# Finishing batches inside the attention loops, a last projection in three parts, and a first chunk in two loads: two cross-attention layers on one core

## The chip, the core and the metric

The kernel runs on one core of a Trainium2 chip. The core has five engines that run side by side, each through its own queue in order: TensorE (matrix products and transposes, PE in the profile, with its weight loads shown apart as PEld), VectorE (DVE), ScalarE (ACT), GpSimd (POOL) and SyncE (SP, which here only issues DMAs). The metric is the device time of one execution in microseconds; smaller is better.

## What is computed

Eight batches of 100 queries with 1024 features pass through two cross-attention layers against the same 1444 context rows of 512 features. All of it is fp32.

```python
def _L0_xattn_ref(query, key, Wq, bq, Wk, bk, Wv, bv, Wo, bo):
    Q = query @ Wq + bq; K = key @ Wk + bk; V = key @ Wv + bv
    weights = softmax(Q @ K.T * scale, axis=-1)
    return query + (weights @ V) @ Wo + bo

def _L1_xattn_ref(emb, latent, Wq, bq, Wk, bk, Wv, bv, gamma, beta):
    q = emb @ Wq + bq; k = latent @ Wk + bk; v = latent @ Wv + bv
    w = softmax(q @ k.T * scale, axis=1)          # over the 100 queries
    x = w @ v + emb
    return (x - mean(x)) * rsqrt(var(x) + 1e-6) * gamma + beta
```

## The kernel before

The program multiplies weights first (Wq with Wk, Wv with Wo), so that keys and values are never formed: scores are a product with the raw context, and the weighted rows of the raw context are projected afterwards. Large products are made from seven half-size products of sums (`half_product`, line 116, is called by all of them).

The stages in order of time: products of weights (`weight_products` for "qk0", "vo0", "qk1"); queries of layer 0; a loop over the eight batches for layer 0, in which scores of batch b + 2 and weighted rows of batch b alternate on TensorE; the projection of layer 0; queries of layer 1; the same kind of loop for layer 1 (lines 780 to 818); and the end of the last batch.

TensorE's instructions run in the order in which the program writes them. The other engines' instructions are put in order by a scheduler, which takes the earliest written of those that are ready by its own estimate; that order is then fixed. Semaphores hold an instruction until its inputs are there and its output buffer is free.

*First chunk.* `weight_products` (lines 179 to 287) works on eight chunks, `units[0]` to `units[7]`, of 128 rows: 1024 columns of the left factor (WqT) and 512 of the right one (WkT). For "qk0" the first half of the left columns and all right columns of each chunk are loaded in turn (lines 191 to 194), chunk 0's left half through ACT's queue and all else through SP's; the left factor's second halves follow (lines 195 to 197). The first product X (line 257) takes the first half of the left columns (four blocks of 128) and the first half of the right ones (256) of chunks 0 to 3, the second, Z, those left columns of chunks 4 to 7, and the third, Y, sums that VectorE makes of second halves (lines 259 and 260). On its queue VectorE also has sums of right chunks scaled by a bias (line 254, `accumulate`). Eight matrix products of ones warm the array up (line 87).

*Layer 1's end.* The loop over b runs 48 steps; for b = 6 and b = 7 a step is one product of the weighted rows (line 446). ScalarE then copies these rows from PSUM (line 457), and `weight_totals` (line 617) transposes a row of totals. Batches 0 to 4 are projected together after b = 4's rows are there, at the end of the loop of b = 5 (`project1_halves`, G1 = 5); batches 5 and 6 together by `project1` at the end of b = 6; batch 7 by `project_last`. A projected batch is ended by `finish`: TensorE transposes eight blocks of it into two banks of PSUM, VectorE adds the value bias from there (line 689) and takes statistics (lines 694 and 699), GpSimd takes the power -0.5 (line 702), VectorE scales and shifts (lines 703 and 707), and GpSimd issues the output (line 708). Batches 0 and 1 are finished at the end of b = 5, batches 2, 3 and 4 at the end of b = 6 ahead of `project1`, and 5 and 6 behind it.

`bank` hands out six banks of PSUM in turn to transposes, totals and projections; a bank can be written again when its reader, mostly VectorE, is done. Rows `z` have three buffers.

Of the kernel before, what the change touches and what calls it, by code (L numbers as in the profile page):

```python
# [24 lines left out]
F32 = mybir.dt.float32  # L25
AF = mybir.ActivationFunctionType
ALU = mybir.AluOpType
# [23 lines left out]
def two_layer_cross_attention(ctx: ExitStack, tc: tile.TileContext, a: dict, out: bass.AP):  # L51
# [127 lines left out]
    def weight_products(name, left, right, l_width, r_width, scaled):  # L179

        H, lh, rh = EC // 2, l_width // 2, r_width // 2
        nb, per = lh // P, 512 // rh
        lsrc = a[left].rearrange("(p c) n -> p c n", c=EC)
        rsrc = a[right].rearrange("(p c) n -> p c n", c=EC)
        units = [unit(f"{name}_{h}") for h in range(EC)]
        if name == "qk0":  # L190
            for h in range(EC):
                first = h == 0
                (nc.scalar if first else nc.sync).dma_start(out=units[h][:, :lh], in_=lsrc[:, h, :lh])
                nc.sync.dma_start(out=units[h][:, l_width:], in_=rsrc[:, h, :])
            for i in range(H):
                for h in (i, H + i):
                    nc.sync.dma_start(out=units[h][:, lh:l_width], in_=lsrc[:, h, lh:])
        else:
            for h in range(EC):
                nc.sync.dma_start(out=units[h][:, :l_width], in_=lsrc[:, h, :])  # L200
                nc.sync.dma_start(out=units[h][:, l_width:], in_=rsrc[:, h, :])

        def lefts(k, j):
            return [units[k * H + i][:, j * lh : (j + 1) * lh] for i in range(H)]

        def rights(k, j):
            return [units[k * H + i][:, l_width + j * rh : l_width + (j + 1) * rh] for i in range(H)]

        A11, A12, A21, A22 = lefts(0, 0), lefts(1, 0), lefts(0, 1), lefts(1, 1)
        B11, B12, B21, B22 = rights(0, 0), rights(0, 1), rights(1, 0), rights(1, 1)  # L210
        extra = [work.tile([P, LC * G1 * T], F32, tag="AT", name=f"{name}_s{n}", bufs=2) for n in range(2)]
        S1 = [extra[i // 2][:, i % 2 * 768 : i % 2 * 768 + lh] for i in range(H)]
        T1 = [extra[i // 2][:, i % 2 * 768 + lh : (i % 2 + 1) * 768] for i in range(H)]

        dst = weights.tile([P, l_width // P, r_width], F32, tag="w", name=name)

        def pair(n):
            return [(bank2 if n == "w" else bank)(f"{name}_{n}{j}") for j in range(2)]

        def product(banks, lhs, rhs, fresh):  # L220
            half_product(banks, lhs, rhs, fresh, nb, rh)

        def block(r, c, j):

            n = r * nb + j * per
            return dst[:, n : n + per, c * rh : (c + 1) * rh]

        def put(r, c, banks):
            for j in range(2):
                nc.scalar.copy(block(r, c, j), banks[j].rearrange("p (n w) -> p n w", n=per))  # L230

        def add(r, c, banks):
            for j in range(2):
                to = block(r, c, j)
                nc.vector.tensor_tensor(to, to, banks[j].rearrange("p (n w) -> p n w", n=per), ALU.add)

        accs = {}

        def accumulate(side):
            for v, of in scaled:  # L240
                if of != side:
                    continue
                width = (l_width, r_width)[side]
                if width == E:
                    acc = row(f"{name}_{v}")
                else:
                    acc = work.tile([P, L], F32, tag="half", name=f"{name}_{v}", bufs=1)
                accs[v] = acc
                for h in range(EC):
                    src = units[h][:, :l_width] if side == 0 else units[h][:, l_width:]  # L250
                    if h == 0:
                        nc.vector.tensor_scalar(acc, src, cols[v][:, h : h + 1], None, ALU.mult)
                    else:
                        nc.vector.scalar_tensor_tensor(acc, src, cols[v][:, h : h + 1], acc, ALU.mult, ALU.add)  # L254

        X = pair("x")
        product(X, A11, B11, True)
        put(0, 0, X)
        combine(T1, B12, B11, ALU.subtract)
        combine(S1, A21, A22, ALU.add)  # L260
        Z = pair("z")
        product(Z, A12, B21, True)
        accumulate(1)
        add(0, 0, Z)
        Y = pair("y")
        product(Y, S1, T1, True)
        put(1, 1, Y)
        combine(B11, B22, T1, ALU.subtract)
        T2 = B11
        combine(B21, B21, T2, ALU.subtract)  # L270
        W = pair("w")
        product(W, A22, B21, True)
        put(1, 0, W)
        combine(S1, S1, A11, ALU.subtract)
        S2 = S1
        combine(B12, B22, B12, ALU.subtract)
        product(X, S2, T2, False)
        put(0, 1, X)
        accumulate(0)
        combine(A21, A11, A21, ALU.subtract)  # L280
        combine(A12, A12, S2, ALU.subtract)
        product(X, A21, B12, False)
        add(1, 0, X)
        add(1, 1, X)
        product(Y, A12, B22, False)
        add(0, 1, Y)
        return dst, [accs[v] for v, _ in scaled]
# [377 lines left out]

        seven_products("o1", A, Bs, S, T_, 4, n, add, add, right=lambda k: right_sums(Bs, T_, (k,)))

    def project1(b0, n, A):

        t0, t1 = b0 * T, (b0 + n) * T  # L670
        for e in range(EC):
            ps = bank(f"o1_{b0}_{e}")
            for k in range(LC):
                nc.tensor.matmul(
                    ps[:, : n * T], wv1[:, k, e * P : (e + 1) * P], A[:, k, : n * T], start=(k == 0), stop=(k == LC - 1)
                )
            to = xT[:, e, t0:t1]
            nc.vector.tensor_tensor(to, to, ps[:, : n * T], ALU.add)

    def untransposed(s):  # L680

# [6 lines left out]
            half = slice(j * 512, (j + 1) * 512)  # L688
            nc.vector.scalar_tensor_tensor(z[:, half], bv1[:T, half], s["r"], ps[:T, :], ALU.mult, ALU.add)

    def statistics(s, j):
        if j == 0:
            s["stats"] = small.tile([T, 2, 6], F32, tag="stats", name=f"stats_{s['b']}")
        nc.vector.bn_stats(s["stats"][:, j, :], s["z"][:, j * 512 : (j + 1) * 512])

    def normalise(s):
        b, z = s["b"], s["z"]
# [12 lines left out]
    def finish(s):  # L710
        untransposed(s)
        for j in range(2):
            statistics(s, j)
        normalise(s)

    def project_last(s, A):

        for j in range(2):
            ps = bank(f"ol_{j}")
            half = slice(j * 512, (j + 1) * 512)  # L720
            for k in range(LC):
                nc.tensor.matmul(ps[:T, :], A[:, k, :T], wv1[:, k, half], start=(k == 0), stop=(k == LC - 1))
            nc.vector.tensor_tensor(s["z"][:, half], s["z"][:, half], ps[:T, :], ALU.add)
            statistics(s, j)
        normalise(s)


# [49 lines left out]
    c1.append(key_bias1(1))  # L777
    weight_sums(batches[0])
    A1 = {}
    for b in range(B):  # L780
        nxt = b + 2 < B
        if b in (0, G1, B - 1):
            n = {0: G1, G1: 2, B - 1: 1}[b]
            t = work.tile([P, LC * G1 * T], F32, tag="AT", name=f"A1T_{b}", bufs=2)
            t = t[:, : LC * n * T].rearrange("p (c t) -> p c t", c=LC)
            for i in range(n):
                A1[b + i] = (t, t[:, :, i * T : (i + 1) * T])
        c, *cT = loaded(load_rows(b), *([load_columns(b + 2)] if nxt else []))
        if nxt:
            A = attend1(batches[b], c)  # L790
            s1 = scores1(batches[b + 2], *cT, c1[(b + 2) // G])
        else:
            A = weighted_rows(batches[b]["w"], c, A1[b][1], f"A1_{b}")
            s1 = iter(())
        for n in range(MC * LC):
            next(s1, None)
            next(A)
            if n == 10 and 1 <= b <= B - 2:
                attended(batches[b - 1], A1[b - 1][1])
        weight_totals(batches[b])  # L800
        if b == B - 1:
            untransposed(batches[b])
        if b + 1 < B:
            weight_sums(batches[b + 1])
        if b == 1:
            AS = project1_sums(wv1)
        if b == G1:
            project1_halves(*AS, A1[0][0])
            for d in range(2):
                finish(batches[d])  # L810
        if b == B - 2:
            for d in range(2, G1):
                finish(batches[d])
            project1(G1, 2, A1[G1][0])
            for d in range(G1, B - 1):
                finish(batches[d])
        if b == B - 1:
            project_last(batches[b], A1[b][0])

# [23 lines left out]
```

## Time and profile before

| | us |
|---|---|
| median of 3 runs (666.31 to 668.25) | 666.34 |
| the profiled execution | 666.33 |
| its span, first to last instruction | 664.4 |
| first matrix product starts | 5.22 |
| first `finish` starts on TensorE | 604.44 |
| loop of batch 6 on TensorE, its totals | 617.33 |
| loop of batch 7 on TensorE, its totals | 647.47 |
| last matrix product ends | 655.59 |

A line of the profile's timeline gives the start and the length in us, the engine, the line of the kernel, the operation, what it writes and reads, shapes, a count, and in brackets the idle time of the engine ahead of it and what ended it. A line of the waits gives who waited for whom, the sum in us, how often, and the longest. One matrix product of fp32 is two instructions in the trace; a transpose is one. POOL's spans are rough. The engines' busy shares are means over the whole span and hide what a stage is limited by.

### The profile page before, as it was taken

The page shows a single profiled execution, that of the slowest core. Times are in us where ns is not written, and L with a number is a line of the kernel's source. Part 1 is how long each engine was busy: PE and PEld are TensorE (multiplying, and loading weights), DVE is VectorE, ACT ScalarE, POOL GpSimd, SP SyncE. Part 2 cuts the span into 40 slices and gives each one's busy share as a digit, 9 for nine tenths or more (in the row PEclk, how much of TensorE's full clock was granted, in tenths as well). Part 3 has the DMA queues.
Part 4 walks back from the last instruction along what each step waited for, and adds up shares of the span by engine and source line. Part 5 has one row for each costly group of instructions (what it writes and reads, how often), then busy time and mean ns, then how long its engine had stood idle before and what let it go on. Part 6 is the DMA issues. An engine that isn't in the chain of part 4 may idle for free.

```text
span 664.4 us, 10317 instructions
## 1 busy us (share of the span) xinstructions
PE 651.4 (98%) x4352; PEld 551.6 (83%) x4352; DVE 359.2 (54%) x649; ACT 101.2 (15%) x295; POOL 22.8 (3%) x31
## 2 busy tenths in 40 slices
PE   9999999999999999999999999999999999999894
PEld 8885445568899999999998555589999999989891
DVE  5979638996055123321232874269344443468884
ACT  1110100331101111101120000213322323210000
POOL 2000000000000000000000000000000000001330
PEclk9999999999999999999999999999999999999998
DMA  9936046000199688888999003038899889900221
GB/s 298 373 117 265 0 135 239 1 0 1 48 340 316 247 291 291 299 288 304 326 331 325 2 0 127 1 111 260 289 312 308 290 292 315 316 15 12 64 75 49
DMA packets 59946, 127.51 MB, mean 192 GB/s; under 512 B 3896, under 2 KB 22328, under 8 KB 59900
## 3 DMA queue, kind: packets, MB, share of 16 engines
q1 hardware_dynamic: 57598, 119.82, 52.9%
q0 software_dynamic: 2048, 6.56, 3.0%
q8 instruction: 34, 0.56, 0.4%
q10 hardware_dynamic: 254, 0.47, 0.2%
q14 instruction: 12, 0.10, 0.0%
HBM read 123.56 MB, written 3.28 MB: 191 GB/s over the span
## 4 chain that ended last, share of the span: by engine, by line
PE 95%; DVE 2%; DMA 1%; issue 0%; POOLq 0%; POOL 0%; DVEq 0%
PE A L446 15%; PE s L476 12%; PE s L573 11%; PE A L629 10%; PE qk_x L116 6%; PE g_x L116 5%; PE qk_y L116 4%; PE o_x L116 4%; PE g_y L116 3%; PE vo_x L116 3%; PE o_y L116 3%; PE qk_w L116 2%; PE qk_z L116 2%; PE vo_y L116 2%; PE g_w L116 2%; PE g_z L116 2%
## 5 line engine op out<-in xcount | busy, mean ns | idle before, releaser
L446 PE MATMUL A<-w,c 120*128 120x100 f32 x960 | 145.4, 268 | 0.0
L446 PEld LDWEIGHTS A<-w,c 120*128 120x128 f32 x960 | 128.6, 191 | 0.1
L573 PE MATMUL s<-g1T,cT 128*120 128x100 f32 (+1 forms) x768 | 123.2, 261 | 0.0
L476 PE MATMUL s<-cT,g0T 128*100 128x131 f32 (+1 forms) x704 | 122.8, 275 | 0.0
L629 PE MATMUL A<-c,w 120*100 120x128 f32 (+1 forms) x576 | 110.7, 273 | 0.0
L573 PEld LDWEIGHTS s<-g1T,cT 128*120 128x120 f32 (+1 forms) x768 | 105.1, 185 | 0.6 <-issue 0.3
L476 PEld LDWEIGHTS s<-cT,g0T 128*100 128x100 f32 x704 | 87.7, 167 | 0.0
L629 PEld LDWEIGHTS A<-c,w 120*100 120x100 f32 (+1 forms) x576 | 74.0, 168 | 0.0
L488 DVE TENSOR_SCALAR p<-s,c 100x394 f32<-100x394 f32 (+2 forms) x32 | 18.8, 594 | 89.6 <-PE s L476 89.4
L593 ACT ACTIVATE w<-w,negmax 120x100 f32<-120x100 f32 (+1 forms) x96 | 35.1, 366 | 75.3 <-DVE negmax L591 75.3
L583 DVE SCALAR_TENSOR_TENSOR w<-s,c 120x400 f32<-120x400 f32 (+1 forms) x24 | 13.8, 573 | 41.6 <-PE s L573 41.6
L116 PE MATMUL qk_x<-qk 128*128 128x256 f32 x128 | 28.9, 384 | 0.4 <-DMA qk<-in_L_xattn_WkT 0.4
L116 PEld LDWEIGHTS qk_x<-qk 128*128 128x128 f32 x128 | 24.2, 192 | 4.7 <-DMA qk<-in_L_xattn_WqT 0.6
L508 ACT COPY w<-pT 120x400 f32<-120x400 f32 (+1 forms) x24 | 11.6, 493 | 100.0 <-PE pT L507 100.0
L702 POOL TENSOR_TENSOR rstd<-rstd,mhalf 100x1 f32<-100x1 f32 x8 | 11.8, 1478 | 233.7 <-DVE rstd L701 233.7
L596 DVE RECIPROCAL rtotal<-total 120x4 f32<-120x4 f32 (+1 forms) x24 | 4.2, 176 | 28.2 <-ACT w L593 28.2
L492 ACT ACTIVATE p<-p,negmax 100x1444 f32<-100x1444 f32 x8 | 12.0, 1499 | 47.2 <-DVE negmax L490 47.2
L515 DVE TENSOR_TENSOR xT<-xT,o_x 128x400 f32<-128x400 f32 (+1 forms) x24 | 13.7, 602 | 8.3 <-PE o_x L116 8.0
L254 DVE SCALAR_TENSOR_TENSOR qk_L_xattn_bk<-qk,L_xattn_bk,qk_L_xattn_bk 128x1024 f32<-128x1024 f32 x14 | 17.9, 1279 | 0.0
L593 ACT ACTIVATION_READ_ACCUMULATOR w<-w,negmax 120x1 f32 (+1 forms) x96 | 17.9, 186 | 0.0
L610 DVE TENSOR_REDUCE part<-w 120x100 f32<-120x1100 f32 x8 | 17.2, 2147 | 0.0
L319 DVE SCALAR_TENSOR_TENSOR kb<-xT,wqbk,kb 128x400 f32<-128x400 f32 x28 | 16.9, 628 | 0.2
(198 smaller groups left out, 861.3 us busy)
## 6 DMA issues: line engine op xcount, KB each, us to landing
c<-in_ctx SPq DMA_DIRECT2D x48, 768.0 KB, 7.8
cT<-in_ctxT SPq DMA_DIRECT2D x32, 728.0 KB, 7.0
cT<-in_ctxT SPq DMA_DIRECT2D x32, 722.0 KB, 6.5
c<-in_ctx SPq DMA_DIRECT2D x16, 512.0 KB, 8.2
qk<-in_L_xattn_WkT SPq DMA_DIRECT2D x16, 256.0 KB, 6.3
vo<-in_L_xattn_Wo SPq DMA_DIRECT2D x8, 512.0 KB, 7.2
qk<-in_L_xattn_WqT SPq DMA_DIRECT2D x8, 512.0 KB
qk<-in_L_xattn_WqT SPq DMA_DIRECT2D x15, 256.0 KB, 5.4
```

Source lines behind the costliest of these rows:

```text
L116: nc.tensor.matmul(banks[n // per][:, n % per * width : (n % per + 1) * width], lhs[i][:, n * P : (n + 1) * P], rhs[i], start=(fresh and i ...
L254: nc.vector.scalar_tensor_tensor(acc, src, cols[v][:, h : h + 1], acc, ALU.mult, ALU.add)
L319: nc.vector.scalar_tensor_tensor(acc, src, wqbk[:, k : k + 1], acc, ALU.mult, ALU.add)
L446: nc.tensor.matmul(ps[:, k * T : (k + 1) * T], c[m // CQ][:r, m % CQ, k * P : (k + 1) * P], w[:r, m, :], start=(m == 0 and k == 0), stop=( ...
L476: nc.tensor.matmul(banks[n // PM][:T, CUTS[n] - o : CUTS[n + 1] - o], q0[:, k, t0 : t0 + T], cT[k][:, CUTS[n] : CUTS[n + 1]], start=(k == ...
L488: nc.vector.tensor_scalar(p[:, o:e], ps[:T, : e - o], SCALE, c0[:, b : b + 1], ALU.mult, ALU.add)
L515: nc.vector.tensor_tensor(to, to, ps[:, : n * width].rearrange("p (n t) -> p n t", n=n), ALU.add)
L573: nc.tensor.matmul(ps[:r, (m - m0) * T : (m - m0 + 1) * T], cT[m // CQ][:, k, o : o + r], q1[:, k, t0 : t0 + T], start=(k == 0), stop=(k = ...
L583: nc.vector.scalar_tensor_tensor(w[:r, grp, :], ps[:r, :GT].rearrange("p (c t) -> p c t", t=T), SCALE, c1[:r, t0 : t0 + T].unsqueeze(1).to ...
L593: nc.scalar.activation(w[:r, m, :], w[:r, m, :], AF.Exp, bias=negmax[:r, m : m + 1], accum_out=total[:r, m : m + 1])
L610: nc.vector.tensor_reduce(part[:MR], w[:MR, :last, :].rearrange("p c t -> p t c"), AX.X, ALU.add)
L629: nc.tensor.matmul(ps[:T, part], w[:r, m, :], c[m // CQ][:r, m % CQ, part], start=(m == 0 and k == 0), stop=(m == MC - 1), skip_group_chec ...
```

## The change

Three edits are made.

1. `finished` names the steps at which batches are finished. In the loop of b = 6 batches 0, 1, 2 and 3 come behind steps 0, 12, 26 and 40; batch 4 comes in the middle of `project1`, behind its fourth block of columns; batches 5 and 6 come behind steps 0 and 16 of the loop of b = 7. The calls at the loops' ends go.
2. `project_last` makes columns 0 to 511, 512 to 895 and 896 to 1023 one after the other, each with its add and statistics, in place of two halves.
3. For "qk0" chunk 0's left half is loaded by two DMAs of 256 columns on ACT's queue; its right half by two DMAs of 256 columns on SP's, the second of which comes behind chunk 1's loads.

```diff
         if name == "qk0":
-            for h in range(EC):
-                first = h == 0
-                (nc.scalar if first else nc.sync).dma_start(out=units[h][:, :lh], in_=lsrc[:, h, :lh])
+            for part in (slice(0, lh // 2), slice(lh // 2, lh)):
+                nc.scalar.dma_start(out=units[0][:, part], in_=lsrc[:, 0, part])
+            nc.sync.dma_start(out=units[0][:, l_width : l_width + rh], in_=rsrc[:, 0, :rh])
+            for h in range(1, EC):
+                nc.sync.dma_start(out=units[h][:, :lh], in_=lsrc[:, h, :lh])
                 nc.sync.dma_start(out=units[h][:, l_width:], in_=rsrc[:, h, :])
+                if h == 1:
+                    nc.sync.dma_start(out=units[0][:, l_width + rh :], in_=rsrc[:, 0, rh:])
...
-    def project1(b0, n, A):
+    def project1(b0, n, A, between):
...
             nc.vector.tensor_tensor(to, to, ps[:, : n * T], ALU.add)
+            if e == EC // 2 - 1:
+                between()
...
-    def statistics(s, j):
+    def statistics(s, j, part, parts):
         if j == 0:
-            s["stats"] = small.tile([T, 2, 6], F32, tag="stats", name=f"stats_{s['b']}")
-        nc.vector.bn_stats(s["stats"][:, j, :], s["z"][:, j * 512 : (j + 1) * 512])
+            s["stats"] = small.tile([T, parts, 6], F32, tag=f"stats{parts}", name=f"stats_{s['b']}")
+        nc.vector.bn_stats(s["stats"][:, j, :], s["z"][:, part])
...
-        for j in range(2):
+        parts = (slice(0, 512), slice(512, 896), slice(896, E))
+        for j, part in enumerate(parts):
+            n = part.stop - part.start
             ps = bank(f"ol_{j}")
-            half = slice(j * 512, (j + 1) * 512)
             for k in range(LC):
-                nc.tensor.matmul(ps[:T, :], A[:, k, :T], wv1[:, k, half], start=(k == 0), stop=(k == LC - 1))
-            nc.vector.tensor_tensor(s["z"][:, half], s["z"][:, half], ps[:T, :], ALU.add)
-            statistics(s, j)
+                nc.tensor.matmul(ps[:T, :n], A[:, k, :T], wv1[:, k, part], start=(k == 0), stop=(k == LC - 1))
+            nc.vector.tensor_tensor(s["z"][:, part], s["z"][:, part], ps[:T, :n], ALU.add)
+            statistics(s, j, part, len(parts))
...
+    finished = {(B - 2, n): (d,) for d, n in enumerate((0, 12, 26, 40))}
+    finished.update({(B - 1, 0): (G1,), (B - 1, 16): (G1 + 1,)})
...
                 attended(batches[b - 1], A1[b - 1][1])
+            for d in finished.get((b, n), ()):
+                finish(batches[d])
...
             project1_halves(*AS, A1[0][0])
-            for d in range(2):
-                finish(batches[d])
         if b == B - 2:
-            for d in range(2, G1):
-                finish(batches[d])
-            project1(G1, 2, A1[G1][0])
-            for d in range(G1, B - 1):
-                finish(batches[d])
+            project1(G1, 2, A1[G1][0], lambda: finish(batches[G1 - 1]))
```

More of the change, by code (lines that the diff above doesn't have):

```diff
@@ L712, in finish @@
         for j in range(2):
-            statistics(s, j)
+            statistics(s, j, slice(j * 512, (j + 1) * 512), 2)
         normalise(s)
     def project_last(s, A):
-        for j in range(2):
+        parts = (slice(0, 512), slice(512, 896), slice(896, E))
+        for j, part in enumerate(parts):
+            n = part.stop - part.start
             ps = bank(f"ol_{j}")
-            half = slice(j * 512, (j + 1) * 512)
             for k in range(LC):
-                nc.tensor.matmul(ps[:T, :], A[:, k, :T], wv1[:, k, half], start=(k == 0), stop=(k == LC - 1))
-            nc.vector.tensor_tensor(s["z"][:, half], s["z"][:, half], ps[:T, :], ALU.add)
-            statistics(s, j)
+                nc.tensor.matmul(ps[:T, :n], A[:, k, :T], wv1[:, k, part], start=(k == 0), stop=(k == LC - 1))
+            nc.vector.tensor_tensor(s["z"][:, part], s["z"][:, part], ps[:T, :n], ALU.add)
+            statistics(s, j, part, len(parts))
         normalise(s)
```

## The prediction

> **What bounds the kernel now.** I read the page's table of engines first, then the waits of TensorE's weight loads over the last 60 us, then the timeline of that stretch, and last the chain of waits at both ends.
>
> ```profile
> PE 651.4 (98%) x4352; PEld 551.6 (83%) x4352; DVE 359.2 (54%) x649; ACT 101.2 (15%) x295; POOL 22.8 (3%) x31
> ```
>
> TensorE is busy for 98% of the span, so a change that adds and removes no matrix work can win only where TensorE stands: before its first product (5.2 us), after its last one (664.4 - 655.6 = 8.8 us), and in holes. Holes are read from the weight loads, because the modelled ends of matmuls cover a part of them. From the first transpose of `finish` (604.44) to the last batch's totals (647.47):
>
> ```profile
> PEld o L674 <- DVE xT L678: 2.0, 1, 2.0
> PEld o L674 <- DVE z L689: 1.1, 1, 1.1
> PEld z L687 <- DVE xT L678: 0.6, 1, 0.6
> ...
> 604.44:647.47 43.03, 40.28 (x319) 38.70 (x318) 39.40 (x67) 0.99 (x2) 14.39 (x14) 1.00 0.19 58
> ```
>
> These are all holes of the stretch: 1.07 + 1.97 + 0.57 = 3.61 us, every one ended by VectorE. The windows row (length; busy PE, PEld, DVE, ACT, POOL) has VectorE busy 39.40 of 43.03 us: here it is nearly as full as TensorE. The timeline gives its price of a finished batch:
>
> ```profile
> 617.64 0.49 ACT L457 COPY A1T<-A 128x400 f32<-128x400 f32 x1 [7.77 <-PE A L446]
> 617.74 0.29 DVE L619 TENSOR_REDUCE r<-wsum_ps 100x1 f32<-100x124 f32 x1 [1.31 <-PE wsum_ps L617]
> ...
> 620.70 0.73 DVE L689 SCALAR_TENSOR_TENSOR z<-L_xattn_bv,r,z 100x512 f32<-100x512 f32 x1
> 621.35 0.20 DVE L699 BATCH_NORM_AGGREGATE mv<-stats 100x2 f32<-100x12 f32 x1
> ...
> 622.14 1.27 DVE L703 SCALAR_TENSOR_TENSOR z<-z,mv,L_xattn_gamma 100x1024 f32<-100x1024 f32 x1
> ...
> 625.73 0.73 DVE L689 SCALAR_TENSOR_TENSOR z<-L_xattn_bv,r,z 100x512 f32<-100x512 f32 x1
> ```
>
> From 620.70 to 625.73 one batch takes 5.03 us of VectorE when the next one fills its gaps. Before that VectorE idles 1.31 us (616.43 to 617.74), since batch 2 is not transposed until the loop of batch 6 ends; then three batches and eight adds of the projection come at once: 618.18 + 3 x 5.03 + 8 x 0.29 = 635.6, and the last add does end at 635.8. The two ends:
>
> ```profile
> 0.75 4.34 DMA qk<-in_L_xattn_WkT
> 5.22 7.48 PE qk_x L116 x32
> ...
> 12.00 0.75 DVE L254 SCALAR_TENSOR_TENSOR qk_L_xattn_bq<-qk,L_xattn_bq,qk_L_xattn_bq 128x512 f32<-128x512 f32 x1 [0.80 <-DMA qk<-in_L_xattn_WkT]
> ...
> 18.55 0.68 DVE L127 TENSOR_TENSOR qk_s<-qk,qk 128x512 f32<-128x512 f32 x1
> ...
> 19.28 0.79 PEld L116 LDWEIGHTS qk_y<-qk_s 128*128 128x128 f32 x4
> ```
> ```profile
> 655.62 0.69 DVE L723 TENSOR_TENSOR z<-z,ol 100x512 f32<-100x512 f32 x1 [2.02 <-PE ol L722]
> 656.35 0.69 DVE L694 BATCH_NORM_STATS2 stats<-z 100x6 f32<-100x512 f32 x1
> 657.08 0.21 DVE L699 BATCH_NORM_AGGREGATE mv<-stats 100x2 f32<-100x12 f32 x1
> ```
>
> The first product waits for the first WkT chunk; but the third one (qk_y) starts at 19.28, right as VectorE's sum for it ends (18.55 + 0.68 = 19.23), and VectorE has run without a gap since 12.00, when the fifth WkT chunk landed.
>
> **What the Trainium skill says.** "Trainium Kernel Development and Optimization", Performance Expectations: matmul busy time is a bad measure, weight-load busy a good one. The trace agrees: in the stretch above PE shows 2.75 us not busy, against 3.61 us of holes before weight loads. "TensorE: Matmul & The Clock Gate", Part 1: the array runs at half speed until it has been busy for about 3.4 us, in a window that runs freely. It agrees: the 16 warm-up instructions last 3.78 us, and the first product takes 7.48 us where the next takes 6.91. The same title as first, Key Constraints: DMAs of all queues share 16 engines; issuing from several saves issue time alone. So splitting a chunk moves no more bytes, it only reorders them; the trace has the engines full from 4 us on. "VectorE: DVE Perf Modes", Why PSUM operands drop a tier: fp32 from PSUM goes at the plain rate, so an add has a fixed part and a part by column. Agrees: 0.346 us for 200 columns (L678), 0.69 for 512.
>
> **Part 1: batches finished in the loops.** TensorE's work is the same (56 transposes, 192 of line 446, 64 of line 674), in another order. Pitches from weight loads: line 446 8.34/74 = 0.1127 us, a transpose 1.85/16 = 0.1156 (0.925 a batch), line 674 5.40/32 = 0.169. From 604.44: the loop of batch 6 is 96 x 0.1127 = 10.82, the four transposes of `attended` 0.37, four batches 3.70: it ends at 619.3. Batches 0 to 3 come to VectorE at about 605.4, 609, 613 and 617.
>
> What goes: the idle 1.31 us of VectorE, and most waits behind the burst. What comes:
> - A new wait. Before, the 24 transposes of batches 2 to 4 lie behind the loop's end and cover ScalarE's copy of the weighted rows (ends 618.13; the totals' transpose ended 617.44). Now `project1` comes at once and needs that copy: 0.7 to 0.8 us, I take 0.76. Queued behind it: o0 to o3, nothing else of weight, since VectorE has a backlog then.
> - VectorE's sum to the last projection add: from 605.44, five batches 25.15, eight adds 2.32, totals 0.2, and gaps of the first batch, which has no neighbour yet, about 0.5: 633.6. TensorE wants it for batch 5's second four transposes at 619.3 + 0.76 + 5.40 + 0.925 + 5.40 + 0.225 + 0.46 = 632.5. It waits 1.1 us.
> - PSUM's ring of six banks: o4 takes o0's bank at about 626.4, and o0's add comes behind batch 3, at 626 or so. Nothing, or the same lag shown one place earlier.
> - Row buffers (3): batch 3 reuses batch 0's, whose output is issued near 611.5 and lands 3.2 us later, before 617. POOL's queue keeps its order (power, output). Nothing.
> - In the loop of batch 7 the transposes of 5 and 6 move behind its first and 17th product; VectorE ends batch 6 near 645, before the last one needs it. The totals and eight transposes of batch 7 still cover the copy there.
>
> Holes 0.76 + 1.1 = 1.9 in place of 3.61: **gain 1.7**. Bounds: 2.85 if VectorE is never late (0.76 left), 0.3 if its fixed order leaves 1.4 us more idle.
>
> **Part 2: three parts of the last projection.** TensorE: 16 instructions of 512 columns at 0.429 become 8 of 512, 8 of 384 (0.32 each) and 8 of 128; no row has the last, the nearest is a 128-column transpose (0.116). Sum 3.43 + 2.57 + 0.92 = 6.92 against 6.86: costs 0.06. VectorE, by 0.344 us per 312 columns: 384 take 0.55, 128 take 0.27; each follows the other 0.04 later. After part two's end: 0.03 + 0.55 + 0.04 + 0.55 + 0.04 + 0.27 + 0.04 + 0.27 + 0.04 = 1.83; part three ends 0.92 after part two, so the aggregate starts 0.91 after TensorE's end, now 657.08 - 655.59 = 1.49. **Gain 0.58 - 0.06 = 0.5**; bounds 0.35 (a fixed part larger in the statistics) and 0.65 (add and statistics of different parts overlap). Power, scale, shift and output behind it are unchanged.
>
> **Part 3: first chunk in two steps.** ACT issues one more load (0.4 us; its first copy is at 11.87), SP one more, and the second half of WkT's chunk goes behind chunk 1: later SP loads are issued one turn (about 0.4 us) later, and the ninth load already waits for an old one to land (it goes at 4.91, as the first lands). The first product could start behind the warm-up, near 4.65 in place of 5.22; at the half clock until about 5.6 that wins 0.35 to 0.4. But qk_y doesn't come earlier than VectorE's sum, and that is counted from the fifth WkT chunk, with the same bytes ahead of it. Narrower rows: no row of 1 KB exists here; by two-kilobyte packets (84 ns) and 1456-byte ones (62 ns) two halves cost some 8 ns more, 16 such per engine, 0.13 us. So the start's gain is spent waiting ahead of qk_y: **-0.1**, bounds -0.7 (VectorE's order puts one operation more ahead of the sum) and +0.35 (the sum comes earlier too).
>
> **Sum.** 1.7 + 0.5 - 0.1 = 2.1. The profiled execution took 666.33 us (span 664.4), the median 666.34, so no correction: 664.2.
>
> **Rivals.**
> 1. VectorE's queue is badly ordered; little gain in the middle: 0.3 + 0.5 - 0.2 = 0.6, so 665.7. For it: no stretch of before shows a batch finished inside such a loop. Against: in 617 to 636 its gaps were filled well. Chance 0.24.
> 2. The start pays too: + 0.35 and 1.9 in the middle, 2.75: 663.6. Against: qk_y's start at 19.28. Chance 0.14.
> 3. Slower. VectorE works in order; if first evictions of the next batch are put ahead of the tail of the one before (3.8 us), it stands until TensorE has transposed, at positions 12, 26 and 40 of the loop. At worst three tails are left at 617.3: 617.3 + 1.3 + 11.3 + 5.0 + 2.3 = 637.2; batch 5 then waits 4.7, with the copy's 0.76 that is 5.5 against 3.61: -1.9, + 0.5 - 0.1, so 667.8. It decides once more than 3 us of idle are put in. Chance 0.10, 0.07 of it over the bound.
>
> **Numbers.** The forecast has 0.52. A measurement of this kernel tells from no change what exceeds 0.3%, 2.0 us: below 664.34 is faster. The forecast lies on that line: 0.34 of its 0.52 below, all of rival 2: faster 0.48; slower 0.07; same 0.45. Range: gain 0.4 to 3.3, 663.0 to 665.9.
>
> **What would show it.** Right: no hole of VectorE at 616 to 618; a hole of 0.7 us before line 674's first weight load, ended by ScalarE; one of about 1 us before a transpose of batch 5; qk_x near 4.7 but qk_y still near 19.3; the aggregate 0.9 us behind the last product. Wrong: VectorE waiting for transposes in the loop of batch 6; qk_y starting at 18.9 or after 19.6; holes at line 674 over 1.5 us.

## The result, and the profile after

The changed kernel takes 663.6 us (median of 6 runs, 663.12 to 664.74), the kernel before on the same chip 666.41: ratio 0.9955, 95% interval 0.9942 to 0.9968. The profiled execution took 663.64 us with a span of 661.7; the span fell by 664.37 - 661.68 = 2.69 us. The forecast was 664.2 with a gain of 2.1; the medians differ by 2.8. The page's line of engines hardly shows it, as TensorE's work is nearly the same (651.4 us before):

```profile
PE 650.8 (98%) x4360; PEld 552.8 (84%) x4360; DVE 359.8 (54%) x651; ACT 101.1 (15%) x295; POOL 22.8 (3%) x31
```

*The middle.* The waits of the weight loads (engine, who was waited for, sum, times, longest), 603 to 648 us:

```profile
PEld z L693 <- DVE xT L682: 1.5, 1, 1.5
...
PEld o L678 <- ACT A1T L461: 0.7, 1, 0.7
```

Two holes in place of three, and one is of a new kind, ended by ScalarE. The windows row of the stretch from the first product of batch 6's loop to batch 7's totals (length; busy PE, PEld, DVE, ACT, POOL):

```profile
604.51:645.45 40.94, 39.23 (x318) 38.70 (x317) 39.48 (x67) 0.98 (x2) 13.91 (x13) 1.00 0.19 61
```

It is 40.94 us, where it was 43.03, with VectorE's work the same (39.48 for 39.40): VectorE now works in what was idle time. The timeline, line by line:

```profile
619.06 0.16 PEld L621 LDWEIGHTS wsum_ps<-ident,wsum 124*100 124x100 f32 x1
...
619.37 0.49 ACT L461 COPY A1T<-A 128x400 f32<-128x400 f32 x1 [10.33 <-PE A L450]
...
619.91 5.37 PEld L678 LDWEIGHTS o<-A1T,wv 128*128 128x128 f32 x32 [0.70 <-ACT A1T L461]
...
631.81 0.78 PEld L693 LDWEIGHTS z<-ident,xT 128*100 128x100 f32 x7
...
633.67 0.35 DVE L682 TENSOR_TENSOR xT<-xT,o 128x200 f32<-128x200 f32 x1
...
634.08 0.12 PEld L693 LDWEIGHTS z<-ident,xT 128*100 128x100 f32 x1 [1.49 <-DVE xT L682]
```

The totals' transpose has nothing behind it that could run beside ScalarE's copy, so the projection stands for 0.70 us. At 631.81 seven of batch 5's eight transposes pass, and the eighth waits 1.49 us until VectorE's last add ends (633.67 + 0.35 = 634.02).

*The start.* In this execution the chain of waits of the changed kernel (start, length, what) no longer runs through the first two products, and the weight loads of the third, qk_y (the line apart, from the timeline), stand for 0.45 us until VectorE's sum is there:

```profile
5.03 6.97 DMA qk<-in_L_xattn_WkT
...
12.10 0.75 DVE qk_L_xattn_bq L258
...
18.73 0.61 DVE qk_s L127
...
19.39 7.17 PE qk_y L116 x32
26.56 6.91 PE qk_w L116 x32
```
```profile
19.38 4.61 PEld L116 LDWEIGHTS qk_y<-qk_s 128*128 128x128 f32 x22 [0.45 <-DVE qk_s L127]
```

The first product begins at 4.63 in place of 5.22, but the fourth, qk_w, at 26.56 (before: 26.51): the third waits for VectorE, which has waited for the fifth WkT chunk.

*The end*, timeline of VectorE:

```profile
652.76 0.56 DVE L730 TENSOR_TENSOR z<-z,ol 100x384 f32<-100x384 f32 x1 [1.16 <-PE ol L729]
653.35 0.56 DVE L700 BATCH_NORM_STATS2 stats<-z 100x6 f32<-100x384 f32 x1
653.83 0.27 DVE L730 TENSOR_TENSOR z<-z,ol 100x128 f32<-100x128 f32 x1
654.13 0.29 DVE L700 BATCH_NORM_STATS2 stats<-z 100x6 f32<-100x128 f32 x1
654.46 0.24 DVE L705 BATCH_NORM_AGGREGATE mv<-stats 100x2 f32<-100x18 f32 x1
```

From the totals (645.45) to the aggregate it is 9.01 us, before 657.08 - 647.47 = 9.61. So: the start loses 0.07 (604.51 against 604.44), the middle wins 2.09, the end 0.60, and what comes behind the aggregate 0.07: 2.69.

### The profile page after: what moved, and what is told of

It is laid out like the page before. It is cut to its first block, busy times and chain, and to the rows that moved or that the text cites. A ratio compares the mean times of both kernels' runs of the same rounds, so it can differ in the third digit from the quotient of the medians.

```text
span 661.7 us, 10338 instructions
## 1 busy us (share of the span) xinstructions
PE 650.8 (98%) x4360; PEld 552.8 (84%) x4360; DVE 359.8 (54%) x651; ACT 101.1 (15%) x295; POOL 22.8 (3%) x31
## 4 chain that ended last, share of the span: by engine, by line
PE 91%; DVE 5%; DMA 1%; issue 1%; SPq 1%; POOL 0%; POOLq 0%; DVEq 0%
PE A L450 14%; PE s L480 12%; PE s L577 12%; PE A L633 10%; PE qk_x L116 5%; PE g_x L116 5%; PE qk_y L116 4%; PE o_x L116 4%; PE g_y L116 3%; PE vo_x L116 3%; PE o_y L116 3%; PE qk_w L116 2%; PE vo_y L116 2%; PE g_w L116 2%; PE g_z L116 2%; PE o_w L116 1%
```

## The experiments

The theory to be tested is that VectorE's lag alone ends the holes of the middle, that the end is a chain of VectorE, and that the early start is lost before the third product. All times are compared with the kernel before on the same chip, five rounds each. For each run the table gives, from its profile, the start of qk_w in the chain of waits, the time from the last weight load of the half-products' projection to batch 7's totals ("middle": 43.24 before, 41.15 after), and from the totals to the aggregate (worked out from unrounded times).

| run | ratio (95%) | span | qk_w | middle | aggregate |
|---|---|---|---|---|---|
| before | 1 | 664.4 | 26.51 | 43.24 | 9.61 |
| after | 0.9955 (0.9942 to 0.9968) | 661.7 | 26.56 | 41.15 | 9.00 |
| e1 loops alone | 0.9973 (0.9962 to 0.9983) | 661.8 | 26.03 | 41.15 | 9.61 |
| e2 three parts alone | 0.9989 (0.9981 to 0.9997) | 664.0 | 26.61 | 43.24 | 9.01 |
| e3 two loads alone | 1.0006 (0.9998 to 1.0014) | 664.6 | 26.78 | 43.24 | 9.61 |
| e4 two batches moved | 0.9970 (0.9959 to 0.9982) | 662.3 | 26.46 | 41.17 | 9.61 |
| e5 copy covered | 0.9997 (0.9983 to 1.0011) | 665.3 | 26.57 | 44.79 | 9.00 |
| e6 batch 4 late | 0.9944 (0.9931 to 0.9956) | 660.7 | 26.61 | 39.69 | 9.47 |
| e7 e5 and e6 | 0.9936 (0.9924 to 0.9948) | 659.9 | 26.52 | 38.97 | 9.48 |
| e8 before, fewer sums | 1.0001 (0.9993 to 1.0009) | 665.0 | 27.19 | 43.24 | 9.61 |
| e9 after, fewer sums | 0.9957 (0.9945 to 0.9969) | 661.7 | 26.59 | 41.15 | 9.01 |
| e10 batch 5 later | 0.9941 (0.9928 to 0.9953) | 660.1 | 26.43 | 39.72 | 9.00 |
| e11 e10 and e5 | 0.9929 (0.9916 to 0.9943) | 659.6 | 26.63 | 39.00 | 9.00 |

**Each part alone.** In e1 the loads and the last projection are as before, in e2 only `parts` is changed, in e3 only the loads.

> The batches finished inside the loops, nothing else of the change. Theory (VectorE's lag is the only thing that ends the holes): the span falls by 2.0 to 2.2 us against the kernel before, the totals of batch 7 come about 2.1 us earlier than 647.47, with the same two holes as in the changed kernel, 0.7 us before the projection of 5 and 6 and 1.5 us in the transposes of batch 5. Rival (part of the middle's gain comes from the start or the end): under 1.7 us.

> The last projection in three parts, nothing else of the change. Theory: the aggregate starts 0.6 us earlier after the last totals, and the span falls by 0.6 to 0.7 us. Rival (the end is bound by something behind the aggregate): under 0.3 us.

> The first chunk in two steps, nothing else of the change. Theory (the third product waits for VectorE's sum): the first product starts at 4.4 instead of 5.2, but the third one between 19.3 and 19.5 as before, and the span is 0.0 to 0.15 us longer. Rival (the early start carries through): the span is 0.3 to 0.4 us shorter.

The middle of e1 is that of the changed kernel to the hundredth, and so is the end of e2: these two parts are independent and carry the whole gain. The span of e1 fell by 2.5 us rather than 2.1 because this execution's start happened to be 0.48 us earlier (26.03; more on it below, with e8); what the loops won is 43.24 - 41.15 = 2.09. The medians of e2 and of the kernel before differ by 0.62 us, as expected. e3 begins its first product early (4.63), but its third starts at 19.61, again behind VectorE's sum (19.55), and qk_w at 26.78; its time is not told apart from no change, and nothing of an early start is left.

**Only batches 2 and 3 moved (e4).**

```diff
+    finished = {(B - 2, 26): (2,), (B - 2, 40): (3,)}
...
-            for d in range(2, G1):
+            for d in range(4, G1):
```

> Only batches 2 and 3 are moved, behind steps 26 and 40 of the loop of batch 6; 0 and 1, and 4, 5 and 6 stay where they were before; the other two parts of the change are left out. Theory (what counts is that VectorE no longer idles at 616 to 618 and has less in hand when the projection starts): most of the gain of the middle, 1.4 to 2.0 us of span. Rival (the spreading of 4, 5 and 6 is what pays): under 0.8 us.

It gives the whole gain of the middle, 2.07 of 2.09. Its holes, from the waits of the weight loads:

```profile
PEld o L674 <- DVE xT L678: 1.0, 1, 1.0
PEld z L689 <- DVE xT L678: 0.6, 1, 0.6
```

So giving VectorE two batches while it was idle is what pays; spreading the others (0, 1, 4, 5 and 6) wins nothing more in the places chosen, as it trades these two holes, and some shorter waits behind them, for the two of the changed kernel.

**The copy covered (e5).** Batch 3 is finished behind the totals of batch 6.

```diff
-    finished = {(B - 2, n): (d,) for d, n in enumerate((0, 12, 26, 40))}
+    finished = {(B - 2, n): (d,) for d, n in enumerate((0, 12, 26))}
...
+        if b == B - 2:
+            finish(batches[3])
```

> The changed kernel with batch 3 finished behind the totals of batch 6 instead of step 40, so that its transposes lie beside ScalarE's copy. Theory (VectorE bounds the stretch): the hole of 0.7 us before the projection is gone, and the one at batch 5's transposes grows from 1.5 to about 2.2 us; the span is within 0.2 us of the changed kernel's 661.7. Rival (TensorE's own path bounds it): the span falls by 0.6 to 0.7 us.

The waits moved as expected, though the second by more (2.54 for 2.2), and yet the kernel loses what it had won: of its 14 times five lie at 663.6 to 665.0 and nine at 666.9 to 669.0 (the ratio in the table is of all 14). The profile is one of the longer ones. Timeline of the weight loads, then windows (length, PEld busy, granted clock, DMA share, GB/s):

```profile
632.70 0.12 PEld L693 LDWEIGHTS z<-ident,xT 128*100 128x100 f32 x1 [0.93 <-DVE xT L682]
634.44 0.12 PEld L693 LDWEIGHTS z<-ident,xT 128*100 128x100 f32 x1 [1.61 <-DVE xT L682]
...
639.93 1.70 PEld L693 LDWEIGHTS z<-ident,xT 128*100 128x100 f32 x8
```
```profile
632.00:636.00 4.00, 1.68 (x16) 0.99 0.12 35
636.00:642.00 6.00, 5.96 (x30) 0.50 0.15 49
```

The copy's hole is gone, the holes at batch 5 grew to 0.93 + 1.61 = 2.54 us (1.49 before the edit), only one weight load apart, and from 636 to 642 the granted clock is 0.50: eight transposes take 1.70 us instead of 0.90. "TensorE: Matmul & The Clock Gate" of the Trainium skill, Part 1, says that the clock falls to a half after an idle window of about 3.4 us, in a window that runs freely. That fits times of two kinds for one kernel, but here the array was not idle for such a time: the clock fell behind 2.54 us of holes, with weight loads busy for 42% of 4 us. In the kernel before the emptiest 4 us (627.15 to 631.15) have 2.03 us of weight loads, and its clock did not fall. The mean granted clock of every execution is on record: 0.996 or 0.997 in the five shorter ones (the other kernels have 0.995 to 0.998), and 0.988 to 0.993 in the nine longer ones. So the longer time goes with the lower clock in all 14, and the five with the full clock have a median of 663.96 us, near the changed kernel's 663.6. The size fits too: the half clock lasts from 635.9 to 642.8, and 6.8 us at half speed cost 3.4; with 2.54 - 0.70 - 1.49 = 0.35 us of holes more that makes some 3.75, and the middle grew by 3.64. What a stretch must be like for the clock to fall was not tested.

**Batch 4 or batch 5 elsewhere (e6, e10), and each with the copy covered (e7, e11).** e6 and e7 do batch 4 in the loop of batch 7; e10 and e11 leave it in the projection and only put 5 and 6 later.

```diff
-    finished.update({(B - 1, 0): (G1,), (B - 1, 16): (G1 + 1,)})
+    finished.update({(B - 1, 0): (G1 - 1,), (B - 1, 14): (G1,), (B - 1, 28): (G1 + 1,)})    # e6, e7
+    finished.update({(B - 1, 18): (G1,), (B - 1, 32): (G1 + 1,)})                           # e10, e11
```

> The changed kernel with batch 4 behind step 0 of the loop of batch 7, and 5 and 6 behind steps 14 and 28. Theory (batch 5 waits because VectorE does batch 4 ahead of the last adds of the projection): the hole of 1.5 us at batch 5 goes, and the span falls by 1.2 to 1.5 us to about 660.3; VectorE then ends batch 6 near the time that batch 7's transposes come. Rival (VectorE has too much in the loop of batch 7): its lag comes back at the last projection, and the span falls by less than 0.5 us.

> Both edits, batch 3 behind the totals of batch 6 and batch 4 in the loop of batch 7. Theory: both holes go, span 1.9 to 2.2 us below the changed kernel's, about 659.6. Rival (VectorE's work from 605 on, some 38 us, is then the longer path): the span stays 0.5 us or more above that.

> The changed kernel with batches 5 and 6 behind steps 18 and 32 of the loop of batch 7 in place of 0 and 16; batch 4 stays in the middle of the projection. Theory (it is batch 5's place, not batch 4's, that makes TensorE wait): the hole of 1.5 us goes, from the last half-product to batch 7's totals it is 39.7 us in place of 41.15, and since VectorE is busy with batch 4 while the projection's last blocks run, the aggregate comes 9.0 us behind the totals; span 660.2. Rival (batch 4 in the middle delays the adds past step 18 as well, or VectorE's lag reaches the end): a hole of over 0.3 us stays, or the aggregate comes 9.4 us or more behind the totals.

> The same with batch 3 finished behind the totals of batch 6 as well, so that its transposes lie beside ScalarE's copy. Theory: no hole is left, 39.0 us from the last half-product to the totals, the aggregate 9.0 us behind them, span 659.4. Rival: as VectorE's work is the longer path now, the span is 659.9 or more, and the clock may fall as it did with the two holes of the earlier run with batch 3 moved.

Each removes the hole of 1.49 us, and with it the covered copy pays in full: the middle goes 41.15, 39.7, 39.0, and in e11 weight loads leave no hole (windows row, as above, over its whole middle):

```profile
604.35:643.35 39.00, 39.00 (x320) 38.92 (x319) 36.73 (x63) 0.99 (x2) 12.45 (x12) 1.00 0.17 54
```

What tells e6 from e10 is the end, where the aggregate comes 9.47 us behind the totals in place of 9.00. Timeline of VectorE there, two lines of e6 and then one of e10:

```profile
651.34 0.56 DVE L730 TENSOR_TENSOR z<-z,ol 100x384 f32<-100x384 f32 x1 [1.79 <-PE ol L729]
651.81 1.15 DVE L700 BATCH_NORM_STATS2 stats<-z 100x6 f32<-100x512 f32 x2
```
```profile
649.33 0.69 DVE L700 BATCH_NORM_STATS2 stats<-z 100x6 f32<-100x512 f32 x1
```

It is no lag of VectorE: in both the first part's add ends about 5.5 us behind the totals, and then VectorE idles until the second part's product. In e10 the first part's statistics fill that time; in e6 the fixed order has them behind the second part's add, so VectorE stands for 1.79 us with them in hand and makes two statistics in a row at 651.81. e7 has the same order and the same end (9.48). Why the scheduler chose it with batch 4 late is not shown.

The forecasts of e10 and e11 came out (39.72 and 39.00, 9.00 for both, spans 660.1 and 659.6). e6 fell 1.0 us below the changed kernel's span where 1.2 to 1.5 were expected, and e7 1.8 where it was 1.9 to 2.2; in both the end took 0.47 of it, and not for the rivals' reason, too much work for VectorE. e11 has the lowest time, 661.49 us against 666.25, ratio 0.9929; its interval overlaps those of e6, e7 and e10, so that its place ahead of them rests on the profiles.

**The start with less to do for VectorE (e8, e9).**

```diff
-                for h in range(EC):
+                for h in range(1 if name == "qk0" and side == 1 else EC):
```

> The kernel before, with seven of the eight chunks left out of the bias sum over WkT's rows in the first product of weights, so that VectorE has about 4.6 us less to do ahead of the sums for the third product. Theory: TensorE's products now follow one another; as the first one starts at 5.2 as before, the third starts at 19.23 in place of 19.28, and the span changes by 0.1 us at most. Rival (VectorE's backlog costs more later on): over 0.3 us shorter.

> The changed kernel with the same seven chunks left out of that sum. Theory (only VectorE's sum keeps the early start from paying): the third product starts at 18.9 in place of 19.38, the span is 0.35 to 0.45 us below the changed kernel's 661.7. Rival (the loads bound the third product too): it starts at 19.3 or later, and the span is the same within 0.1 us.

e9 speaks against the word "only" of the theory; its time can't, as 0.4 us would be 0.0006 of the ratio. Timeline of its weight loads, one row of its products (PE) and VectorE's sums:

```profile
6.63 1.59 PEld L116 LDWEIGHTS qk_x<-qk 128*128 128x128 f32 x8 [0.74 <-issue]
...
8.46 1.59 PEld L116 LDWEIGHTS qk_x<-qk 128*128 128x128 f32 x8 [0.24 <-issue]
...
10.70 0.42 DVE L127 TENSOR_TENSOR qk_s<-qk 128x256 f32<-128x256 f32 x1 [1.89 <-DMA qk<-in_L_xattn_WkT]
10.78 1.59 PEld L116 LDWEIGHTS qk_x<-qk 128*128 128x128 f32 x8 [0.72 <-issue]
10.81 1.97 PE L116 MATMUL qk_x<-qk 128*128 128x256 f32 x8 [0.35 <-DMA qk<-in_L_xattn_WkT]
12.40 6.88 PEld L116 LDWEIGHTS qk_z<-qk 128*128 128x128 f32 x32
...
17.67 0.69 DVE L127 TENSOR_TENSOR qk_s<-qk,qk 128x512 f32<-128x512 f32 x1
19.30 4.72 PEld L116 LDWEIGHTS qk_y<-qk_s 128*128 128x128 f32 x22
```

VectorE's sum is there at 18.36, a microsecond early, and qk_y still starts at 19.30. The first product now stops ahead of its second, third and fourth chunk (0.74, 0.24, 0.72 us before the weight loads; the row of the products at 10.81 names the DMA of WkT). So there are two walls, chunks that land 1.8 to 2.3 us apart, and VectorE's sum. In this execution the chunks alone keep qk_y near 19.3; in the changed kernel's the sum alone did, by 0.45 us. Which one counts differs from one execution to the next: with the start of the changed kernel the chain runs through the sum in three profiles (the changed kernel, e3, e5), through the fourth WkT chunk in e6 and e7, and through an unbroken first product in e10 and e11, and qk_w starts at 26.43 to 26.78 in all of them.

e8 shows neither wall, but a third thing. Its sum ends at 18.56, and yet the weight loads of qk_y begin at 19.91, as its first product took 8.12 us (7.48 before) from the same start. That is the half clock of the start: the weight loads of qk_x come 0.43 us apart until about 7.1 us and 0.22 apart behind that, while in the kernel before the change comes at about 5.8; from 6 to 7 us there are three of them in e8 and six before. In e1, whose start was early, they are 0.22 apart nearly from the first one on (4.93), and its WkT chunks also landed 0.3 to 0.6 us earlier than in the kernel before. So when the clock becomes full varies between executions, and one profile of a start can lie half a microsecond or more off another for this reason. e8's time is not told apart from that of the kernel before.

## Why the prediction was right

- **The bound.** "A change that adds and removes no matrix work can win only where TensorE stands": held in all parts; the middles of e1 to e11 differ by holes and short waits alone, apart from the clock in e5.
- **The new wait at the copy**: forecast 0.76 us, measured 0.70. **Its relief of VectorE**: the loop of batch 6 was to end at 619.3, it ended at 619.06.
- **Batch 5's wait**: last add forecast at 633.6, TensorE's arrival at 632.5. The add started at 633.67, ended at 634.02, and TensorE, there at 632.6, had waited for 1.49 us where 1.1 was forecast: VectorE's sum came out 0.4 too small.
- **Gain of the middle**: 1.7 forecast, 2.09 measured. The term that was mis-sized is the one to be removed, "These are all holes of the stretch: ... 3.61 us". They were more: in the kernel before, transposes of batches 5 and 6 came one by one behind adds, in waits too short for the timeline to set apart:

```profile
634.76 2.03 PEld L687 LDWEIGHTS z<-ident,xT 128*100 128x100 f32 x13 [0.57 <-DVE xT L678]
```

Thirteen weight loads in 2.03 us, at 0.156 each; undisturbed ones take 0.1156, so 0.5 us more of waiting. 3.61 + 0.5 - 0.70 - 1.49 = 1.9, near the 2.09 measured. e11, whose middle has no hole, gives the whole: 43.24 - 39.00 = 4.24 us of waiting before, and 41.15 - 39.00 = 2.15 after. Both sides of the prediction's sum were too small (3.61 for 4.24, 1.9 for 2.15), and the two errors partly cancelled; that much was luck.
- **The end**: 0.5 forecast, 0.60 measured, within its bounds. Adds and statistics were priced at 0.55 (384 columns) and 0.27 (128); they took 0.56 and 0.27 to 0.29, and the overlap that was named as the upper bound came: the last add starts 0.48 after the statistics ahead of it, which take 0.56.
- **The start**: -0.1 forecast, -0.07 in the profile, an agreement that is chance, as starts of kernels with one load spread over more than 1 us (26.03 to 27.19); e3 (0.9998 to 1.0014) doesn't resolve it, but gives no room for rival 2's + 0.35. The reason given, VectorE's sum counted from the fifth WkT chunk, is what the chain shows in the changed kernel's profile; that the chunks alone can hold it as well (e9, e6, e7) was not foreseen, and the half clock was taken to end at about 5.6.
- **Rival 1 and rival 3** (a badly ordered VectorE): in the loop of batch 6 no wait of VectorE for a transpose shows. The first evictions of the next batch were put ahead of the tail of the one before, as rival 3 feared, yet the transposes were always there in time.

## What to carry to other kernels

When two engines are both nearly full over a stretch, look for the idle time of the one that ends the waits, ahead of the burst, and give it work there: two batches moved 2 to 5 us ahead brought the whole gain of the middle. A hole that moves isn't gone: remove the wait that ends last first (batch 5's place), and only then the one before it (the copy), because in the other order the second hole grew by more than the first one gave (e5: 1.05 us for 0.70). Before loading a first chunk in pieces, follow the chain to the first point that something else sets: if that is another engine's sum or the next chunk's landing, the early start is spent there. And look at the order that a scheduler gave an engine even where it has time: e6 lost 0.47 us at the end to statistics that were put behind a wait.

## What the runs showed beyond that

- Behind two holes of 0.93 and 1.61 us close together TensorE's clock was halved from 636 to 642 us (e5), in nine of 14 executions by their mean clocks; behind holes of 1.07 and 1.97 us in the kernel before, 2.7 us of work apart, it was not.
- The half clock of the start ended between about 4 and 7 us in thirteen profiles, with the same 16 warm-up instructions from 1.06 us on.
- In the profiles qk_w starts at 26.03 to 27.19 with the first chunk in one load (five executions) and at 26.43 to 26.78 with it in two (eight): the median is the same within 0.1 us. The spread is smaller, but the two ends of the first range are e1 and e8, for whose starts the clock accounts at least in part, so the loads are not shown to be the reason.
- Pieces of 384 and 128 columns cost what a straight line through 200 and 512 gives: 0.55 and 0.27 us against 0.56 and 0.27 measured for the add.
